# Summing a Mamba scan's states with TensorE transposes instead of identity products, with half the convolution moved to TensorE

## The chip, the cores and the metric

The kernel runs on one core of one Trainium2 chip. The metric is device microseconds from launch to end; the median of three runs of the kernel before is 8551.73 us (8550.24 to 8556.64). One further execution was taken by the hardware profiler, and all durations below are from it.

## The reference

All tensors are float32. The input is 8 images of 256 channels and 32 x 32 pixels, read as 1024 tokens of 256 channels. Four networks follow each other. The first is four Mamba layers and a gate; the other three are attention blocks, which the change does not touch. A Mamba layer is, for each image (cut to what matters):

```python
xin, z = jnp.split(layernorm(xs) @ iw.T, 2, axis=-1)        # 512 channels each
xin = silu(causal_depthwise_conv(xin, cw, K=4) + cb)
proj = xin @ xw.T                                           # 16 for dt, 16 for B, 16 for C
dt = softplus(proj[..., :16] @ dw.T + db)                   # 512 channels
A = -exp(alog)                                              # 512 x 16
def step(h, t):                                             # 1024 tokens, one after the other
    h = h * exp(dt_t[..., None] * A) + (dt_t * x_t)[..., None] * b_t[:, None, :]
    return (h, einsum('bdn,bn->bd', h, c_t))                # sum over the 16 states
y = ys + xin * D
xs = xs + (y * silu(z)) @ ow.T
```

## The kernel before

**Units and steps.** A unit is one layer, one image and one half of its tokens (512 tokens): 4 x 8 x 2 = 64 units, made at lines 510 to 515. A unit's 512 channels are four blocks of 128, taken as two pairs (`q`, blocks `i` = 0 and 1), and its 16 states are eight groups `g` of two (`j`). A step is one `(q, g)`: 16 steps to a unit, 1024 in all. The main loop (lines 587 to 617) writes the work of one step out part by part, in the order of `PARTS` (line 64). Each engine keeps this written order, so an instruction that waits holds back everything behind it on its engine.

**One step.**
- `bx0` and `bx1` (`forced`, lines 472 to 481, one for each block `i`): TensorE spreads `dt * x * B` over the two states. The matrix `dtxT` holds `dt * x` with tokens on the partitions; `dg` holds B as diagonals. The result `bx` (128 channels x 512 tokens x 2 states) has two PSUM buffers of two banks. The array is used as four tiles of 64 x 64: row tile `h` is a half of the tokens, column tile `r` a half of the channels.
- `da0` and `da1` (line 483): ScalarE computes `da = exp(dt * A)` for the next step, two tiles each.
- `state` (line 528): VectorE runs the recurrence with a hardware scan over 512 tokens, one scan for each block and state, four in a step, into `h`.
- `hc` (`product`, line 540): GpSimd multiplies the four state tiles by C, which a DMA has broadcast to all partitions (`ct`, two steps ahead). In the first half of an image VectorE first copies out the last state as the carry.
- `y` (`summed`, lines 492 to 503), three steps later (`LAG_Y`): TensorE sums the states in PSUM. The multiplied states `h` stream as the moving operand against `twin`, two stacked 64 x 64 identities, in the same 64 x 64 tiles. A pair `q` begins with the products `xin * D` through the diagonals `dd`, and both PSUM banks of `y` gather 16 states.
- `z` (`gate`, line 505): after the last group, VectorE multiplies `y` by `silu(z)` into `sz`.

**Beside the scan.** The letters `a` to `d` in `PARTS` are four slots in each step, 64 slots in a unit. `beside` (line 552) puts the segments of five generators there; `BESIDE_SCAN` (lines 66 to 72) lists the slot of each segment. `inward`, two units ahead, is the layer norm, the input projection (products `pin`), the convolution, SiLU and the projection `pp`. `onward`, one unit ahead, makes dt with softplus and `dtx`; `turn` transposes `dtx`; `outward`, one unit behind, is the output projection `po`; `weights` loads a layer. They share two PSUM banks (the tag `mm`, line 97), so a product waits for an earlier one to be read out.

**Convolution.** For each of four blocks, ScalarE takes the last tap out of PSUM with a scale and a bias (line 249), and VectorE adds the three other taps from the same PSUM tile (lines 253 to 255). GpSimd adds the first three tokens' contribution (line 257).

**Softplus.** The kernel computes it as max(v, 0) + log(1 + exp(-|v|)) with a correction for the rounding of 1 + e. ScalarE makes `e`, `one` = 1 + e, `ln` and 1 - `one`; GpSimd then makes three sums of 128 x 1024: `e + (1 - one)`, `+ ln`, `+ dt` (lines 321 to 325).

The prologue (`PROLOGUE`, line 80) does the same stages for the first units in a written order. Later come the attention blocks, from about 6240 us on.

Of the kernel before, what the change touches and what calls it, by code (L numbers as in the profile page):

```python
# [12 lines left out]
F32 = mybir.dt.float32  # L13
# [6 lines left out]
P = 128  # L20
# [6 lines left out]
NG = 2  # L27
# [25 lines left out]
class Engines:  # L53
# [7 lines left out]
LAG_Y = 3  # L61


PARTS = ("ct", "a", "bx0", "da0", "y", "z", "bx1", "da1", "b", "hc", "c", "d")

BESIDE_SCAN = (
    ("weights", 2, (0, 0, 0, 11)),
    ("onward", 1, (1, 8, 8, 8, 8, 13, 19, 25, 27, 31, 35, 35, 41, 45, 46, 51)),
    ("turn", 1, (46, 49, 57, 58)),
    ("outward", -1, (6, 13, 16, 20, 23, 30, 32, 33, 35, 41, 48, 50, 53, 53, 57)),  # L70
    ("inward", 2, (0, 0, 3, 10, 15, 19, 19, 29, 29, 34, 39, 39, 44, 44, 44, 46, 49, 59, 63)),
)

DIAGONALS = (12, 24, 36, 39, 44, 48, 52, 56)

LAST_ON_VECTOR = (2, 1)

PROLOGUE = "WIIWIZZZWIWWIIIIIIIIIIIIIIIJOJOJOGJOJJOGJOOOJOOJJJTGCOGOJOGCGOJJOOTJDGJJJGTJT"  # L80


def mamba_phase(tc, ctx, a, spill, ident, gvec, stats):
# [43 lines left out]
    def weights(s):  # L127

        l = s["l"]
        if (s["b"], s["c"]) != (0, 0):  # L130
            return
        w = layers[l] = {}
        v = w["vec"] = wp.tile([P, V_N], F32, name=f"vec{l}", tag="vec", bufs=2)
        nc.sync.dma_start(v, a["m_vec"][l])
        w["in"] = wp.tile([P, CT, 2 * DI], F32, name=f"win{l}", tag="win")
        nc.sync.dma_start(w["in"], a["m_in"][l])
        yield
        w["A"] = wp.tile([P, DT * DS], F32, name=f"A{l}", tag="A", bufs=2)
        nc.scalar.activation(w["A"], v[:, V_AL:V_AL + DT * DS], AF.Exp)
        nc.scalar.activation(w["A"], w["A"], AF.Identity, scale=-1.0)  # L140
        yield

        w["dd"] = wp.tile([P, DT, H], F32, name=f"dd{l}", tag="dd", bufs=2)
        for j in range(DT):
            nc.gpsimd.tensor_scalar_mul(w["dd"][:, j, :], twin, v[:, V_D + j:V_D + j + 1])
        yield

        ps = ps_m.tile([P, T], F32, name=f"pib{l}", tag="mm")
        for e in range(2 * DT):
            for k in range(CT):  # L150
# [45 lines left out]
    def inward(s):  # L196
# [34 lines left out]
        if c == 0:  # L231
            tail = st["tail"] = wk2.tile([P, DT, K - 1], F32, name=f"tail{u}", tag="tail")
            head = w["head"]
        else:
            tail = st["tail"]
            head = wk1.tile([P, DT, K - 1], F32, name=f"head{u}", tag="head")
            more = wk1.tile([P, DT, K - 1], F32, name=f"more{u}", tag="more")
            nc.gpsimd.tensor_tensor(head, tail, taps[:, :, 0:1].to_broadcast([P, DT, K - 1]), ALU.mult)
            for k in range(1, K - 1):
                n = K - 1 - k  # L240
                nc.gpsimd.tensor_tensor(more[:, :, :n], tail[:, :, k:], taps[:, :, k:k + 1].to_broadcast([P, DT, n]), ALU.mult)
                nc.gpsimd.tensor_tensor(head[:, :, :n], head[:, :, :n], more[:, :, :n], ALU.add)
        xin = s["xin"] = []
        for q in range(DT // 2):
            xin.append(wk5.tile([P, 2, T], F32, name=f"xin{u}_{q}", tag="xin"))
            for i in range(2):
# [33 lines left out]
    def onward(s):  # L280
# [18 lines left out]
        for q in range(DT // 2):  # L299
# [13 lines left out]
            one = wk1.tile([P, 2, T], F32, name=f"one{u}_{q}", tag="one")  # L313
            nc.scalar.activation(one, e, AF.Identity, bias=1.0)
            yield
            ln = wk1.tile([P, 2, T], F32, name=f"ln{u}_{q}", tag="sq")
            nc.scalar.activation(ln, one, AF.Ln)

            nc.scalar.activation(one, one, AF.Identity, scale=-1.0, bias=1.0)
            yield  # L320
            nc.gpsimd.tensor_tensor(e, e, one, ALU.add)
            yield
            nc.gpsimd.tensor_tensor(e, e, ln, ALU.add)
            yield
            nc.gpsimd.tensor_tensor(dt, dt, e, ALU.add)
            yield
# [145 lines left out]
    def forced(s, q, g, i):  # L472

        bx = ps_b.tile([P, T, NG], F32, name=f"bx{s['name']}_{q}_{g}_{i}", tag="bx")
        for k in range(NB):
            for h in range(2):
                for r in range(2):
                    t = h * (T // 2) + k * H
                    nc.tensor.matmul(bx[r * H:(r + 1) * H, t:t + H, :], lhsT=s["dtxT"][q][h * H:(h + 1) * H, i, k, r * H:(r + 1) * H],
                                     rhs=s["dg"][g][h * H:(h + 1) * H, k, :, :], start=True, stop=True)  # L480
        return bx

    def decays(s, q, g, i):
# [8 lines left out]
    def summed(s, q, g, j, h):  # L492

        if g == 0 and j == 0:
            s["y"] = [ps_y.tile([P, T], F32, name=f"y{s['name']}_{q}_{r}", tag=f"y{r}") for r in range(2)]
            for r in range(2):
# [12 lines left out]

    units = []  # L510
    for l in range(NL):
# [75 lines left out]
    for i in range(len(steps) + per_unit):  # L587
# [6 lines left out]
        for part in PARTS:  # L594
# [15 lines left out]
            elif 0 <= i - LAG_Y < len(steps):  # L610
                s, q, g = steps[i - LAG_Y]
                if part == "y":
                    for j in range(NG):
                        summed(s, q, g, j, hs[i - LAG_Y])
                    del hs[i - LAG_Y]
                elif g == NGR - 1:
                    gate(s, q)


ATT_W = ("wq1", "wk1", "wv1", "wo1", "wq2", "wk2", "wv2", "wq3", "wk3", "wv3", "wo3")  # L620
# [601 lines left out]
def layout(i):  # L1222
# [18 lines left out]


    swap = np.arange(DI).reshape(DT // 2, 2, 2, H).transpose(0, 2, 1, 3).reshape(DI)
    m["in_proj_w"] = np.concatenate([m["in_proj_w"][:, :DI], m["in_proj_w"][:, DI + swap]], axis=1)
# [51 lines left out]
```

## Time and profile before

| | |
|---|---|
| median of three runs | 8551.73 us |
| the profiled execution's span, first to last instruction | 8545.1 us |
| TensorE products (PE) busy | 8295.1 us, 97% |
| TensorE weight loads (PEld) busy | 4184.9 us, 49% |
| VectorE (DVE) busy | 7175.6 us, 84% |
| ScalarE (ACT) busy | 5401.4 us, 63% |
| GpSimd (POOL) busy | 6738.1 us, 79% |
| first `bx` product to last `y` product | 106.2 to about 6242 us |

The profile has the span as the execution's only time; the median is 6.6 us above it. All instructions are recorded through one helper, so every line reads L48, and groups are told apart by their tiles: `y<-h,twin` is the product that writes `y` from `h` and `twin`. A float32 product stands as two MATMUL rows, a transposition as one. A form such as `64*64 64x512` is the tile of the array (rows * columns) and then the moving operand (partitions x columns). In a timeline row the two numbers are the start and the time to the last end, and `x16` is how many instructions were merged. Rows overlap: the next group begins while the last products of the one before are still in the array, so the time of a group is read from its start to the next group's start.

### The profile page before, as it was taken

Reading aid. Unit: us, or ns where it says so; the run is one execution under the profiler, and the core shown is the slowest. Engines: PE = TensorE matmul, PEld = TensorE weight load, DVE = VectorE, ACT = ScalarE, POOL = GpSimd, SP = SyncE. Lnnn points to the kernel's source line nnn. Section 1 sums busy time; section 2 is a strip of 40 time slices with the busy share of each in tenths; the row PEclk is TensorE's granted clock in tenths of the full one; section 3 lists DMA queues with packets and bytes.
Section 4 is the critical chain, followed back from the end, with each engine's and each line's share of the span. In section 5 each row is a group of like instructions: output and inputs, shape, how many; then the busy total and the mean of one; then the engine's idle time right before and its main releaser. Section 6 shows DMA issues by size and latency. Waiting matters only on the chain.

```text
span 8545.1 us, 226062 instructions
## 1 busy us (share of the span) xinstructions
PE 8295.1 (97%) x98322; PEld 4184.9 (49%) x98322; DVE 7175.6 (84%) x7069; ACT 5401.4 (63%) x7613; POOL 6738.1 (79%) x2339
## 2 busy tenths in 40 slices
PE   7999999999999999999999999999989999999998
PEld 4555555555555555555555555555533333333332
DVE  5999999999999999999999999999964555665566
ACT  6777777777777777777777777777632344333434
POOL 5999999999999999999999999999912343334435
PEclk9999999999999999999999999999999999999999
DMA  3444444444443444444444444444410000000000
GB/s 117 128 130 129 129 130 134 132 129 128 128 130 127 135 128 133 128 130 129 128 129 131 130 138 135 141 143 138 142 62 5 9 6 7 10 6 6 1 6 11
DMA packets 558021, 841.07 MB, mean 98 GB/s; under 512 B 311329, under 2 KB 312417, under 8 KB 556385
## 3 DMA queue, kind: packets, MB, share of 16 engines
q1 hardware_dynamic: 556736, 825.47, 31.6%
q8 instruction: 780, 12.78, 0.6%
q14 instruction: 217, 1.77, 0.1%
q10 hardware_dynamic: 288, 1.05, 0.0%
HBM read 771.31 MB, written 55.05 MB: 97 GB/s over the span
## 4 chain that ended last, share of the span: by engine, by line
PE 88%; DVE 6%; ACT 2%; issue 2%; POOL 1%; DMA 0%; SPq 0%; DVEq 0%; POOLq 0%; ACTq 0%
PE bx L48 21%; PE y L48 20%; PE pin L48 11%; PE fs L48 8%; PE fo L48 7%; PE po L48 5%; DVE h L48 4%; PE pp L48 3%; PE fwq L48 2%; PE fwv L48 2%; PE pd L48 2%; PE pvar L48 1%; PE fwk L48 1%; PE pmu L48 1%; PE fpo L48 1%
## 5 line engine op out<-in xcount | busy, mean ns | idle before, releaser
L48 POOL TENSOR_TENSOR h<-h,ct 128x2048 f32<-128x2048 f32 x1022 | 4637.7, 4560 | 169.1 <-DVE hc L48 80.4
L48 ACT ACTIVATE da<-dt,A 128x512 f32<-128x512 f32 x4096 | 2644.6, 715 | 267.2 <-DVE h L48 266.3
L48 PEld LDWEIGHTS bx<-dg,dtxT 64*64 64x64 f32 x65536 | 1889.7, 133 | 1268.8 <-issue 1128.1
L48 DVE TENSOR_TENSOR_SCAN h<-da,hc,bx 128x512 f32<-128x512 f32 x2048 | 2454.7, 1261 | 61.4 <-PE bx L48 29.4
L48 DVE TENSOR_TENSOR_SCAN h<-da,bx 128x512 f32<-128x512 f32 x2048 | 2354.9, 1204 | 95.8 <-PE bx L48 76.8
L48 PE MATMUL bx<-dg,dtxT 64*64 64x128 f32 x65536 | 2222.0, 272 | 64.3 <-DVE h L48 34.7
L48 PE MATMUL y<-h,twin 64*64 64x512 f32 x16384 | 1956.0, 590 | 7.9 <-DVE h L48 4.7
L48 ACT ACTIVATE fp<-fs 128x1024 f32<-128x1024 f32 x768 | 746.3, 1022 | 1117.3 <-PE fs L48 1110.5
L48 PE MATMUL pin<-xn,win 128*128 128x512 f32 x2048 | 1004.9, 614 | 58.8 <-ACT sz L48 48.2
L48 PEld LDWEIGHTS y<-h,twin 64*64 64x64 f32 x16384 | 614.1, 133 | 631.2 <-issue 617.1
L48 POOL TENSOR_TENSOR fz<-fp,fp 128x1024 f32<-128x1024 f32 x48 | 121.9, 2540 | 979.1 <-ACT fp L48 979.1
L48 POOL TENSOR_TENSOR fz<-fz,fp 128x1024 f32<-128x1024 f32 x224 | 586.7, 2622 | 336.6 <-ACT fp L48 332.6
L48 PE MATMUL fo<-fp,fv 128*32 128x512 f32 (+2 forms) x3584 | 781.3, 608 | 4.0 <-ACT fp L48 2.6
L48 DVE TENSOR_TENSOR fz<-fz,fp 128x1024 f32<-128x1024 f32 x384 | 616.8, 1606 | 118.5 <-ACT fp L48 100.7
L48 DVE SCALAR_TENSOR_TENSOR xin<-pin,vec,xin 128x509 f32<-128x509 f32 (+2 forms) x768 | 572.3, 746 | 60.1 <-ACT tail L48 21.2
L48 PE MATMUL fs<-fq,fk 32*128 32x512 f32 (+1 forms) x3072 | 582.2, 634 | 4.1 <-ACT fp L48 2.5
L48 PEld LDWEIGHTS pin<-xn,win 128*128 128x128 f32 x2048 | 349.5, 190 | 423.0 <-issue 281.6
L48 PE MATMUL po<-sz,wo 128*128 128x512 f32 x1024 | 484.1, 605 | 0.8 <-DVE sz L48 0.8
L48 PEld LDWEIGHTS fo<-fp,fv 128*32 128x32 f32 (+2 forms) x3584 | 191.5, 127 | 515.1 <-issue 469.5
L48 ACT ACTIVATE sz<-pin,ib 128x512 f32<-128x512 f32 x256 | 176.0, 688 | 418.3 <-PE pin L48 418.3
L48 ACT ACTIVATE xin<-pin,cb,vec 128x512 f32<-128x512 f32 x256 | 199.2, 778 | 286.0 <-PE pin L48 285.9
L48 POOL TENSOR_TENSOR e<-e,one 128x1024 f32<-128x1024 f32 x128 | 304.5, 2379 | 84.7 <-ACT one L48 81.1
(143 smaller groups left out, 7416.0 us busy)
## 6 DMA issues: line engine op xcount, KB each, us to landing
ct<-cdr SPq DMA_DIRECT2D x1024, 512.0 KB
dg<-diagonals SPq DMA_DIRECT2D x512, 256.0 KB
spill<-xo SPq DMA_DIRECT2D x63, 512.0 KB
x<-spill SPq DMA_DIRECT2D x48, 512.0 KB
xo<-spill SPq DMA_DIRECT2D x48, 512.0 KB
x<-in_x SPq DMA_DIRECT2D x16, 512.0 KB
res<-in_x SPq DMA_DIRECT2D x16, 512.0 KB
diagonals<-bt SPq DMA_DIRECT2D x512, 4.0 KB
```

Of the source, the lines that this page charges most:

```text
L48: return self.tc.keep_in_program_order(getattr(self.engine, name)(*args, **kwargs))
```

## The change

- **States summed by transposes.** `summed` now makes the multiplied states the stationary operand (64 rows of channels, 128 tokens as columns) and streams the 64 x 64 identity past it with `is_transpose`, adding in PSUM. The sum stands with tokens on the partitions: for each state 4 token blocks x 2 blocks `i` x 2 row tiles `r` = 16 transposes. The `xin * D` products take the same shape, with `xin` stationary.
- **Turned back.** After the last group, a new `leave` (part `z`) copies both banks of `y` to SBUF with ScalarE, and `gate` (new part `g`) turns them back by eight 128 x 128 transposes into the same two PSUM banks before VectorE's multiplication.
- **`bx` in 64 x 128 tiles.** `forced` issues one product over all 128 channels where it issued two over 64 each.
- **Half of the convolution on TensorE.** For `q` = 0 (`CONV_Q` = 1) ScalarE copies both projected blocks to SBUF, and four taps are products with diagonal matrices `taps` (made once a layer by GpSimd), shifted in the output columns, into two `mm` banks at once; ScalarE takes the sums out. The second half's first tokens use the kept `past`. The weights' order of channels is changed to fit.
- **Softplus.** `ln` goes to PSUM, 512 tokens at a time, and VectorE adds it to `dt`; GpSimd keeps two of its three sums. `one` uses the buffer `sq`.
- **Order.** `PARTS`, the slots of all stages, those of the DMAs that load the diagonals, and the prologue are new.

```diff
-PARTS = ("ct", "a", "bx0", "da0", "y", "z", "bx1", "da1", "b", "hc", "c", "d")
+CONV_Q = 1
+PARTS = ("bx0", "y", "ct", "z", "g", "da0", "bx1", "a", "da1", "b", "c", "hc", "d")

-    ("onward", 1, (1, 8, 8, 8, 8, 13, 19, 25, 27, 31, 35, 35, 41, 45, 46, 51)),
-    ("turn", 1, (46, 49, 57, 58)),
-    ("outward", -1, (6, 13, 16, 20, 23, 30, 32, 33, 35, 41, 48, 50, 53, 53, 57)),
-    ("inward", 2, (0, 0, 3, 10, 15, 19, 19, 29, 29, 34, 39, 39, 44, 44, 44, 46, 49, 59, 63)),
+    ("onward", 1, (0, 3, 9, 9, 13, 14, 21, 28, 29, 38, 43, 43, 46, 48, 50, 63)),
+    ("turn", 1, (42, 51, 60, 63)),
+    ("outward", -1, (2, 9, 12, 16, 16, 20, 25, 29, 30, 33, 43, 47, 48, 48, 56)),
+    ("inward", 2, (5, 5, 15, 21, 21, 25, 27, 32, 39, 41, 41, 47, 47, 47, 49, 49, 54, 55, 59)),
-DIAGONALS = (12, 24, 36, 39, 44, 48, 52, 56)
+DIAGONALS = (21, 28, 29, 33, 37, 48, 60, 61)

+        w["taps"] = wp.tile([P, 2 * CONV_Q, K, H], F32, name=f"taps{l}", tag="taps")
+        for j in range(2 * CONV_Q):
+            for k in range(K):
+                nc.gpsimd.tensor_scalar_mul(w["taps"][:, j, k, :], twin, v[:, V_CW + j * K + k:V_CW + j * K + k + 1])
...
+            if q < CONV_Q:
+                raw = xin[q]
+                for i in range(2):
+                    j = 2 * q + i
+                    ps = in_proj(j)
+                    nc.scalar.activation(raw[:, i, :], ps, AF.Identity, bias=w["ib"][:, j:j + 1])
+                    yield
+                conv = [ps_m.tile([P, T], F32, name=f"conv{u}_{q}_{r}", tag="mm") for r in range(2)]
+                def tap(k, to, source, stop=False):
+                    for r in range(2):
+                        for i in range(2):
+                            nc.tensor.matmul(conv[r][i * H:(i + 1) * H, to], lhsT=w["taps"][r * H:(r + 1) * H, 2 * q + i, k, :],
+                                             rhs=source(slice(r * H, (r + 1) * H), i), start=(k == K - 1 and to.start == 0), stop=stop)
...
+                for n in range(K):
+                    tap(K - 1 - n, slice(n, T), lambda rows, i: raw[rows, i, :T - n], stop=(c == 0 and n == K - 1))
+                    if n == 1:
+                        yield
+                if c:
+                    past = st["past", q]
+                    for n in range(1, K):
+                        tap(K - 1 - n, slice(0, n), lambda rows, i: past[rows, i, K - 1 - n:], stop=(n == K - 1))
+                for r in range(2):
+                    nc.scalar.activation(xin[q][:, r, :], conv[r], AF.Identity, bias=w["vec"][:, V_CB + 2 * q + r:V_CB + 2 * q + r + 1])
+                yield
+                continue
...
-            ln = wk1.tile([P, 2, T], F32, name=f"ln{u}_{q}", tag="sq")
-            nc.scalar.activation(ln, one, AF.Ln)
+            for r in range(2):
+                ln = ps_m.tile([P, T], F32, name=f"ln{u}_{q}_{r}", tag="mm")
+                nc.scalar.activation(ln, one[:, r, :], AF.Ln)
+                nc.vector.tensor_tensor(dt[:, r, :], ln, dt[:, r, :], ALU.add)
+                yield
...
-            nc.gpsimd.tensor_tensor(e, e, ln, ALU.add)
...
-                for r in range(2):
-                    t = h * (T // 2) + k * H
-                    nc.tensor.matmul(bx[r * H:(r + 1) * H, t:t + H, :], lhsT=s["dtxT"][q][h * H:(h + 1) * H, i, k, r * H:(r + 1) * H],
-                                     rhs=s["dg"][g][h * H:(h + 1) * H, k, :, :], start=True, stop=True)
+                t = h * (T // 2) + k * H
+                nc.tensor.matmul(bx[:, t:t + H, :], lhsT=s["dtxT"][q][h * H:(h + 1) * H, i, k, :], rhs=s["dg"][g][h * H:(h + 1) * H, k, :, :],
+                                 start=True, stop=True)
...
-                    nc.tensor.matmul(s["y"][r][i * H:(i + 1) * H, :], lhsT=s["w"]["dd"][r * H:(r + 1) * H, 2 * q + i, :],
-                                     rhs=s["xin"][q][r * H:(r + 1) * H, i, :], start=True, stop=False)
+                    for r in range(2):
+                        nc.tensor.matmul(s["y"][r][:, k, i, :], lhsT=s["xin"][q][r * H:(r + 1) * H, i, k * P:(k + 1) * P],
+                                         rhs=s["w"]["dd"][r * H:(r + 1) * H, 2 * q + i, :],
+                                         start=(k == 0 and i == 0), stop=False, skip_group_check=True)
+        last = g == NGR - 1 and j == NG - 1
+        for k in range(NB):
+            for i in range(2):
+                for r in range(2):
+                    nc.tensor.matmul(s["y"][r][:, k, i, :], lhsT=h[r * H:(r + 1) * H, i, j, k * P:(k + 1) * P], rhs=twin[r * H:(r + 1) * H, :],
+                                     is_transpose=True, start=False, stop=(last and k == NB - 1 and i == 1), skip_group_check=True)
+    def leave(s, q):
+        s["yt"] = wk1.tile([P, 2, NB, P], F32, name=f"yt{s['name']}_{q}", tag="res")
         for r in range(2):
-            for i in range(2):
-                nc.tensor.matmul(s["y"][r][i * H:(i + 1) * H, :], lhsT=twin[r * H:(r + 1) * H, :], rhs=h[r * H:(r + 1) * H, i, j, :],
-                                 start=False, stop=(g == NGR - 1 and j == NG - 1))
+            nc.scalar.copy(s["yt"][:, r, :, :].rearrange("p b t -> p (b t)"), s["y"][r].rearrange("p b i t -> p (b i t)"))
 
     def gate(s, q):
         for r in range(2):
             z = s["sz"][:, 2 * q + r, :]
-            nc.vector.tensor_tensor(z, s["y"][r], z, ALU.mult)
+            back = ps_y.tile([P, NB, P], F32, name=f"back{s['name']}_{q}_{r}", tag=f"y{r}")
+            for k in range(NB):
+                nc.tensor.transpose(back[:, k, :], s["yt"][:, r, k, :], ident)
+            nc.vector.tensor_tensor(z, back.rearrange("p b t -> p (b t)"), z, ALU.mult)
```

More of the change, by code (lines that the diff above doesn't have):

```diff
@@ L237, in inward @@
             more = wk1.tile([P, DT, K - 1], F32, name=f"more{u}", tag="more")
-            nc.gpsimd.tensor_tensor(head, tail, taps[:, :, 0:1].to_broadcast([P, DT, K - 1]), ALU.mult)
+            J = slice(2 * CONV_Q, DT)
+            N = DT - 2 * CONV_Q
+            nc.gpsimd.tensor_tensor(head[:, J, :], tail[:, J, :], taps[:, J, 0:1].to_broadcast([P, N, K - 1]), ALU.mult)
             for k in range(1, K - 1):
                 n = K - 1 - k
-                nc.gpsimd.tensor_tensor(more[:, :, :n], tail[:, :, k:], taps[:, :, k:k + 1].to_broadcast([P, DT, n]), ALU.mult)
-                nc.gpsimd.tensor_tensor(head[:, :, :n], head[:, :, :n], more[:, :, :n], ALU.add)
+                nc.gpsimd.tensor_tensor(more[:, J, :n], tail[:, J, k:], taps[:, J, k:k + 1].to_broadcast([P, N, n]), ALU.mult)
+                nc.gpsimd.tensor_tensor(head[:, J, :n], head[:, J, :n], more[:, J, :n], ALU.add)
         xin = s["xin"] = []
@@ L245, in inward @@
             xin.append(wk5.tile([P, 2, T], F32, name=f"xin{u}_{q}", tag="xin"))
+            if q < CONV_Q:
[11 more added lines that the diff above has]
+                                             rhs=source(slice(r * H, (r + 1) * H), i), start=(k == K - 1 and to.start == 0), stop=stop)
+                if c == 0:
+                    past = st["past", q] = wk2.tile([P, 2, K - 1], F32, name=f"past{u}_{q}", tag=f"past{q}")
+                    nc.scalar.copy(past, raw[:, :, T - K + 1:])
+                for n in range(K):
[10 more added lines that the diff above has]
+                continue
             for i in range(2):
@@ L312, in onward @@
             nc.scalar.activation(e, e, AF.Exp, scale=-1.0)
[L313 removed]
+            one = wk1.tile([P, 2, T], F32, name=f"one{u}_{q}", tag="sq")
             nc.scalar.activation(one, e, AF.Identity, bias=1.0)
             yield
[L316 to L317 removed]
+            for r in range(2):
+                ln = ps_m.tile([P, T], F32, name=f"ln{u}_{q}_{r}", tag="mm")
+                nc.scalar.activation(ln, one[:, r, :], AF.Ln)
+                nc.vector.tensor_tensor(dt[:, r, :], ln, dt[:, r, :], ALU.add)
+                yield
             nc.scalar.activation(one, one, AF.Identity, scale=-1.0, bias=1.0)
[L320 removed]
             nc.gpsimd.tensor_tensor(e, e, one, ALU.add)
[L322 to L323 removed]
             yield
@@ L494, in summed @@
         if g == 0 and j == 0:
-            s["y"] = [ps_y.tile([P, T], F32, name=f"y{s['name']}_{q}_{r}", tag=f"y{r}") for r in range(2)]
-            for r in range(2):
+            s["y"] = [ps_y.tile([P, NB, 2, H], F32, name=f"y{s['name']}_{q}_{r}", tag=f"y{r}") for r in range(2)]
+            for k in range(NB):
                 for i in range(2):
-                    nc.tensor.matmul(s["y"][r][i * H:(i + 1) * H, :], lhsT=s["w"]["dd"][r * H:(r + 1) * H, 2 * q + i, :],
-                                     rhs=s["xin"][q][r * H:(r + 1) * H, i, :], start=True, stop=False)
+                    for r in range(2):
[10 more added lines that the diff above has]
+        s["yt"] = wk1.tile([P, 2, NB, P], F32, name=f"yt{s['name']}_{q}", tag="res")
         for r in range(2):
-            for i in range(2):
-                nc.tensor.matmul(s["y"][r][i * H:(i + 1) * H, :], lhsT=twin[r * H:(r + 1) * H, :], rhs=h[r * H:(r + 1) * H, i, j, :],
-                                 start=False, stop=(g == NGR - 1 and j == NG - 1))
+            nc.scalar.copy(s["yt"][:, r, :, :].rearrange("p b t -> p (b t)"), s["y"][r].rearrange("p b i t -> p (b i t)"))
     def gate(s, q):
@@ L507, in gate @@
             z = s["sz"][:, 2 * q + r, :]
-            nc.vector.tensor_tensor(z, s["y"][r], z, ALU.mult)
+            back = ps_y.tile([P, NB, P], F32, name=f"back{s['name']}_{q}_{r}", tag=f"y{r}")
+            for k in range(NB):
+                nc.tensor.transpose(back[:, k, :], s["yt"][:, r, k, :], ident)
+            nc.vector.tensor_tensor(z, back.rearrange("p b t -> p (b t)"), z, ALU.mult)
     units = []
@@ L616, in mamba_phase @@
                 elif g == NGR - 1:
-                    gate(s, q)
+                    (leave if part == "z" else gate)(s, q)
 ATT_W = ("wq1", "wk1", "wv1", "wo1", "wq2", "wk2", "wv2", "wq3", "wk3", "wv3", "wo3")
@@ L1243, in layout @@
     swap = np.arange(DI).reshape(DT // 2, 2, 2, H).transpose(0, 2, 1, 3).reshape(DI)
-    m["in_proj_w"] = np.concatenate([m["in_proj_w"][:, :DI], m["in_proj_w"][:, DI + swap]], axis=1)
+    part = np.concatenate([swap[:2 * P * CONV_Q], np.arange(2 * P * CONV_Q, DI)])
+    m["in_proj_w"] = np.concatenate([m["in_proj_w"][:, part], m["in_proj_w"][:, DI + swap]], axis=1)
+    m["conv_w"] = m["conv_w"][:, part]
     m["out_proj_w"] = m["out_proj_w"][:, :, swap]
```

4 lines of the change are left out of this document (2 added, 2 removed).

## The prediction

> **What bounds the kernel now.** I read the page's busy table, then one window from the middle of the scan, then TensorE's timeline, then what TensorE waited for. The page gives TensorE 97%, but this includes the attention blocks. The stretch that the change touches is 1000:5500 (columns: length, then busy time of PE, PEld, DVE, ACT, POOL, then clock):
>
> ```profile
> 1000.00:5500.00 4500.00, 4433.15 (x65211) 2467.72 (x65213) 4245.53 (x4332) 3317.19 (x4919) 4337.13 (x1476) 1.00 0.43 131
> ```
>
> TensorE is busy 98.5%, GpSimd 96.4%, VectorE 94.3%, ScalarE 73.7%, at full clock. GpSimd ran 751 state products there, so a step is 5.99 us and a unit 95.9 us; 64 units after the first `bx` at 106 us end near 6242 us.
>
> ```profile
> 3036.16 1.10 PE L48 MATMUL bx<-dg,dtxT 64*64 64x128 f32 x32
> 3037.08 1.90 PE L48 MATMUL y<-h,twin 64*64 64x512 f32 x16
> 3038.80 1.05 PE L48 MATMUL bx<-dg,dtxT 64*64 64x128 f32 x32
> 3039.96 1.96 PE L48 MATMUL pin<-xn,win 128*128 128x512 f32 x4
> 3042.69 1.98 PE L48 MATMUL pin<-xn,win 128*128 128x512 f32 x4 [0.78 <-ACT sz L48]
> 3044.61 1.10 PE L48 MATMUL bx<-dg,dtxT 64*64 64x128 f32 x32
> 3045.53 1.04 PE L48 MATMUL y<-xin,dd 64*64 64x512 f32 x8
> 3046.39 1.90 PE L48 MATMUL y<-h,twin 64*64 64x512 f32 x16
> 3048.11 1.05 PE L48 MATMUL bx<-dg,dtxT 64*64 64x128 f32 x32
> 3049.09 0.66 PE L48 MATMUL pt<-ident,dtx 128*128 128x128 f32 x4
> ```
>
> The groups stand back to back. From start to start: `bx` 0.92, `y` 1.72 (four rounds of 0.43), `bx` 0.98 where another tile shape follows, `xin * D` 0.86, four transpositions 0.49. Only one wait, 0.78 us, is marked. Its total, with the next largest:
>
> ```profile
> PE pin L48 <- ACT sz L48: 36.6, 47, 0.8
> PE bx L48 <- DVE h L48: 13.8, 51, 0.5
> ```
>
> Over 47 units that is 1.1 us in 95.9. TensorE's work sets the pace, and a saving elsewhere buys at most this 1.1 us. GpSimd (92.4 us a unit) and VectorE (90.5) stand close behind.
>
> **The change part by part, in us of TensorE per unit.** Weight loads price most of it. The first two rows are loads for transpositions; the third is products that move a single column, so that their spacing is that of a plain load:
>
> ```profile
> 2597.53 0.32 PEld L48 LDWEIGHTS pb<-ident,proj 16*128 16x128 f32 x4 [0.17 <-ACT da L48]
> 3049.09 0.42 PEld L48 LDWEIGHTS pt<-ident,dtx 128*128 128x128 f32 x4 [0.17 <-DVE h L48]
> 2990.20 3.63 PE L48 MATMUL pib<-vec,win 128*128 128x1 f32 x32
> 2993.76 1.10 PE L48 MATMUL bx<-dg,dtxT 64*64 64x128 f32 x32
> ```
>
> A load of 128 columns for a transposition follows the last one after (0.32 - 0.137)/3 = 0.061 us (0.137 is one load). A plain float32 load of 128 columns takes (2993.76 - 2990.20)/32 = 0.111. A transposition moving 128 columns takes 0.109 (the `pt` group less its first, exposed load), so moving 64 takes 0.055.
>
> 1. *State sums.* 2 states x 16 transposes are 16 pairs a step, the two row tiles of a pair side by side, as the four tiles are now. A pair costs the larger of its load (0.061) and its product (0.055): I take 0.06. 16 x 0.06 = 0.96, plus 0.05 because `bx`'s plain load no longer fits under the last product: 1.01 in place of 1.72. Over 16 steps **-11.3**. Ends: 0.055 a pair, 1.3 better; 0.111 (loads as slow as plain ones), 13 worse. `pb` has the same tile width and the same kind of load, so I stay near it.
> 2. *`bx` in pairs.* 256 rounds as before, but the load is 0.111 against 0.109 for the product: +0.002 to 0.003 each, +0.7. The first load after a change of tile shape lies open: `pin` x4 takes 1.98 after such a change and 1.88 without, 0.10 for 128 columns, and half of it now for 64; +0.05 x 16 = +0.8. Together **+1.5**; ends 0 and +3.3 (a pair costing 0.007 more).
> 3. *`xin * D`.* 32 instructions, 16 pairs at the plain load's 0.111 = 1.78 against 0.86, twice: **+1.8**.
> 4. *Turning back.* Eight transpositions 0.87, two changes of shape at 0.09 each, and open loads of 0.1: 1.15, twice: **+2.3**.
> 5. *Waiting for the copy.* `z` and `g` stand together, so TensorE holds `bx1` and all behind it while ScalarE copies. `dtxT<-pt` shows the chain: last transposition to its result 0.27, 0.04 to the copy's start, 0.59 the copy; with 0.05 back, 0.9 before the first four can start, and the second copy lets the other four wait another 0.1: **+2.0** for two pairs. Ends: 1.6, and 5.8 if ScalarE were each time in the 1.9 us SiLU of `sz`. `da0` now follows the copies on ScalarE, and VectorE's gate follows `back`; both have room (ScalarE 26%; VectorE's scans of `bx0`, 2.3 us, run meanwhile).
> 6. *Convolution.* Four taps x 2 rounds x 0.43 = 3.44; the three short products of a second half, 6 rounds of about 0.06, in every second unit 0.18; two visits in another tile shape 0.4: **+4.0**.
>
> Sum: -11.3 + 1.5 + 1.8 + 2.3 + 2.0 + 4.0 = **+0.3**.
>
> VectorE loses six convolution passes (0.75 each) and gains four sums (nearest row: `sz<-y,sz`, 0.67): -1.8. GpSimd loses two 2.38 us sums and the `head` edge: -5.0. ScalarE gains four copies (0.59) and two conv read-outs (0.69): +3.8 on 70.7. None of them sets the pace now, and after it VectorE stands at 88.7 and GpSimd at 87.4, so this buys nothing until TensorE has fallen to some 89 us.
>
> *New waits.* VectorE's sum waits for `ln` in ScalarE's order and holds the next scans; `bx` is two buffers ahead, so VectorE's 5.4 idle us cover it. The sum also holds an `mm` bank, and the convolution holds both from slot 32 to 39: in that stretch `onward` (38) and `outward` (33, done by 16 outside the last layer) ask for none. After `ln` (slot 43) the next `mm` product is in slot 47, one step later. `pp` comes one step after the SiLU as now. Slots in GpSimd's queue: `hc` moves behind slot `c`, and the three steps until `y` cover it. SP's queue: `ct` is still sent two steps ahead and the diagonals of the next unit before it begins; DMA share is 43%. I put the change in waits at **+0.3**, between -1.1 (all gone) and +2.0 (two more waits as long as one scan pair can make them). Prologue: eight products of 0.5 on GpSimd and another order, taken as 0, between -5 and +15 us in all.
>
> So **+0.6 us a unit, x 64 = +38 us**. On the profiled span of 8545.1 this is 8583; the median lies 6.6 above the span, so **8590 us**.
>
> [...]
>
> **Rivals.**
> - *The loads hide better (faster).* If a pair of state transposes costs 0.055 (product alone, `pt`'s price per column), step 1 gains 1.3: 0.6 - 1.3 = -0.7, 8507 us. It decides from 0.0577 down (0.6 / 256 below 0.06). For it: `pt`'s loads vanish under 0.109 products. Against: 0.061 in `pb`, and loads of both tiles go on at once. With `bx` at 0.109 as well, -1.4 and 8460. Should all of TensorE's old waits go too, -2.8 and 8370.
> - *Waits take the place of the sum (slower).* Two copies behind a busy ScalarE (+3.8), or `mm` waits of a scan pair twice a unit: +2.5 to +4.5, 8700 to 8850. Against: slots leave a step between holders.
> - *Transposing loads at the plain price, or row tiles not side by side (much slower).* +13 a unit, 9400 us. Against: `pb`; `bx`'s four loads now fit under 0.109.
> - *GpSimd or VectorE take over:* at 89 us a unit, 8110 us; no sum here comes near it, TensorE's best being 95.9 + 0.3 - 1.3 - 1.5 - 0.4 - 1.1 = 91.9 with every bound in its favour.
>
> **How the numbers follow.** Near balance as summed, 8535 to 8700: 0.49. Loads hide better: 0.38. Waits: 0.09. Plain price: 0.04. The range takes the first case's upper bounds (pairs of `bx` 0.007 dearer, or waits +2) to 8700 and the second's to 8430. A measurement here can tell 0.2% (17 us). The first case's lower part, near 8551, and a part of the second's give "same" 0.11; faster 0.40; slower 0.49.
>
> **What would show it.** Right: `y` groups of about 1.0 us start to start with 32 rows; `bx` groups 0.92 to 1.0; two gaps of about 0.9 us a unit ahead of `back`; PE still 97 to 99% busy at 1000:5500 and GpSimd near 91%, VectorE 92%. Wrong: `y` spacing away from 0.06; a clock below 1.00; PE idle on `mm` readers (ACT or DVE) beyond 3 us a unit; a step set by VectorE or GpSimd.

## The result and the profile after

The median of twenty runs is 8565.9 us (8555.7 to 8569.9), against 8550.7 us (8545.1 to 8556.6) for the kernel before, also over twenty runs. The ratio is 1.0017 with a 95% interval of 1.0010 to 1.0023. The kernel is 15 us slower. The sign of the likeliest case was right, its +38 us more than twice too large, and the centre lies inside the 0.2% that I had called "same". The profiled span is 8564.1 us, 19.0 above that of before.

The page after, its busy table:

```profile
span 8564.1 us, 206743 instructions
PE 8299.7 (97%) x88850; PEld 5192.3 (61%) x88850; DVE 7041.0 (82%) x6941; ACT 5553.7 (65%) x8093; POOL 6442.0 (75%) x2179
```

TensorE's busy time is the same as before (8295.1) with different work inside it. VectorE lost 135 us, GpSimd 296 us; neither loss reached the end time. The scan stretch 1000:5500 by windows (columns as before: length, busy time of PE, PEld, DVE, ACT, POOL, clock, DMA share, GB/s):

```profile
1000.00:5500.00 4500.00, 4422.50 (x57985) 3196.99 (x57984) 4126.51 (x4215) 3408.96 (x5239) 4102.30 (x1355) 0.99 0.44 130
```

TensorE 98.3%, VectorE 91.7%, GpSimd 91.2%: the shares that the prediction named (97 to 99, 92, 91). TensorE's timeline of the kernel after, some 15 us later than where the prediction looked at before's:

```profile
3050.86 1.95 PE L48 MATMUL conv<-xin,taps 64*64 64x512 f32 x16
3052.74 1.16 PE L48 MATMUL bx<-dg,dtxT 64*128 64x128 f32 x16
3053.73 1.16 PE L48 MATMUL y<-twin,h 64*128 64x64 f32 x32
3054.72 1.12 PE L48 MATMUL bx<-dg,dtxT 64*128 64x128 f32 x16
3055.77 1.94 PE L48 MATMUL conv<-xin,taps 64*64 64x510 f32 x16
3057.64 1.16 PE L48 MATMUL bx<-dg,dtxT 64*128 64x128 f32 x16
3058.64 1.17 PE L48 MATMUL y<-twin,h 64*128 64x64 f32 x32
3060.47 1.15 PE L48 MATMUL back<-ident,yt 128*128 128x128 f32 x8 [0.67 <-ACT yt L48]
3061.55 0.72 PE L48 MATMUL bx<-dg,dtxT 64*128 64x128 f32 x8
```

From start to start: `y` 0.99 with 32 rows (was 1.72), `bx` 0.99 ahead of `y` (was 0.92) and 1.03 ahead of another tile shape (was 0.98), a convolution visit 1.88, `back` 1.08. Ahead of `back` stands the wait for ScalarE's copy. The two largest waits of TensorE in 1000:5500, after:

```profile
PE back L48 <- ACT yt L48: 62.5, 92, 1.1
PE pib L48 <- DVE dt L48: 6.5, 3, 2.2
```

The wait of `pin` for `sz` (36.6 us before) and that of `bx` for `h` (13.8) are gone. The last line stands for only three events, and much of the result hangs on it.

**Where the time went.** I took each unit's length from one first scan to the next, and each group of TensorE's work from its start to the next group's start, for twelve regular units of layer 2, its third to its fourteenth (us a unit):

| tile | before | after | change | forecast |
|---|---|---|---|---|
| `y` with the wait ahead of `back` | 27.47 | 18.05 | -9.42 | -11.3 + 2.0 |
| `bx` | 30.83 | 33.30 | +2.47 | +1.5 |
| `xin * D` | 1.72 | 3.47 | +1.75 | +1.8 |
| `back` | 0 | 2.15 | +2.15 | +2.3 |
| `conv` | 0 | 3.89 | +3.89 | +4.0 |
| `pin` | 16.04 | 14.53 | -1.51 | } |
| all others | 19.47 | 20.11 | +0.64 | } +0.3 |
| sum | 95.53 | 95.50 | -0.02 | +0.6 |

A regular unit is as long as before, but this hides a loss of clock. Five of the twelve units last 1.5 us longer than their neighbours (96.65 against 95.12, or 96.1 against 94.6). In each of these five, and in none of the other seven, the trace's record of the granted clock has one stretch of 3.4 us at half speed, shortly after the unit's first scan, behind the products `pb` and `pd`. The unit just ahead of the twelve shows one too (windows with the columns as above, then TensorE's timeline):

```profile
3283.00:3293.10 10.10, 10.10 (x152) 7.61 (x151) 8.27 (x9) 10.09 (x18) 9.73 (x3) 1.00 0.43 144
3293.10:3296.50 3.40, 3.40 (x52) 3.40 (x50) 3.01 (x4) 3.40 (x7) 3.09 (x2) 0.51 0.36 105
```
```profile
3291.14 1.70 PE L48 MATMUL pd<-proj,wdt 16*128 16x512 f32 x3
3292.77 1.78 PE L48 MATMUL bx<-dg,dtxT 64*128 64x128 f32 x16
3294.33 1.92 PE L48 MATMUL y<-twin,h 64*128 64x64 f32 x32
3296.04 1.36 PE L48 MATMUL bx<-dg,dtxT 64*128 64x128 f32 x16
```

`y` takes 1.71 here in place of 0.99, and the two `bx` groups 1.56 and 1.29 in place of 0.99 and 1.03, though TensorE had no pause. In the table this is 0.35 us of `bx` and 0.29 of `y`. From the second unit to the sixty-first, the three that load weights left out, there are 23 such stretches in 57 units. At 1.5 us each that is some 35 us, an estimate, and more than the whole difference of 15. The kernel before has none in these units.

Since the regular units balance, the 19.0 us of the span show up elsewhere, and they can be added up: first scan +4.4 (the prologue), layer 0 +7.7, layer 1 +11.1, layer 2 +7.6, layer 3 -12.8, after the last scan +1.0. In layers 0 to 2 one unit, the fifteenth, in which the next layer's weights are loaded, went from 99.0, 99.0 and 102.3 to 107.4, 109.0 and 108.9: +25 us together, almost the whole growth of these three layers. This is the stage (windows 2990:3008, 3008:3026 and 3026:3044 after, columns as above):

```profile
2990.00:3008.00 18.00, 15.55 (x164) 10.40 (x161) 15.43 (x17) 14.13 (x25) 17.95 (x15) 0.91 0.55 109
3008.00:3026.00 18.00, 17.23 (x140) 15.78 (x142) 5.40 (x7) 8.62 (x13) 8.41 (x10) 0.62 0.29 106
3026.00:3044.00 18.00, 18.00 (x212) 12.01 (x210) 16.54 (x20) 8.76 (x15) 15.39 (x4) 1.00 0.37 119
```

The clock is 0.62 in the middle window. TensorE's timeline there, after:

```profile
3004.60 1.98 PE L48 MATMUL po<-sz,wo 128*128 128x512 f32 x4
3008.77 6.05 PE L48 MATMUL pib<-vec,win 128*128 128x1 f32 x32 [2.18 <-DVE dt L48]
3014.76 2.08 PE L48 MATMUL bx<-dg,dtxT 64*128 64x128 f32 x16
3016.62 3.52 PE L48 MATMUL y<-dd,xin 64*128 64x64 f32 x32
3019.93 1.92 PE L48 MATMUL y<-twin,h 64*128 64x64 f32 x32
3021.63 2.00 PE L48 MATMUL bx<-dg,dtxT 64*128 64x128 f32 x16
3023.56 1.98 PE L48 MATMUL po<-sz,wo 128*128 128x512 f32 x4
3025.48 1.16 PE L48 MATMUL bx<-dg,dtxT 64*128 64x128 f32 x16
```

And VectorE's:

```profile
3008.03 0.69 DVE L48 TENSOR_TENSOR dt<-ln,dt 128x512 f32<-128x512 f32 x1 [0.90 <-ACT ln L48]
3016.95 2.33 DVE L48 TENSOR_TENSOR_SCAN h<-da,bx 128x512 f32<-128x512 f32 x2 [8.16 <-PE bx L48]
```

The product `pib` (slot 11 of the unit) needs an `mm` bank. One was held by `po` from slot 9, the other by the first `ln` of the new softplus, also slot 9, which is free only when VectorE has added it at 3008.03. TensorE stands still for 2.18 us and then runs at half speed: `pib` takes 6.0 us where before it took 3.56 in the row that the prediction shows, `bx` 1.86 in place of 0.99, `xin * D` 3.3 in place of 1.73.

### The profile page after: what moved, and what is told of

It is laid out like the page before. It is cut to its first block, busy times and chain, and to the rows that moved or that the text cites. A ratio compares the mean times of both kernels' runs of the same rounds, so it can differ in the third digit from the quotient of the medians.

```text
span 8564.1 us, 206743 instructions
## 1 busy us (share of the span) xinstructions
PE 8299.7 (97%) x88850; PEld 5192.3 (61%) x88850; DVE 7041.0 (82%) x6941; ACT 5553.7 (65%) x8093; POOL 6442.0 (75%) x2179
## 4 chain that ended last, share of the span: by engine, by line
PE 90%; ACT 5%; DVE 3%; issue 1%; POOL 1%; DMA 0%; SPq 0%; DVEq 0%; POOLq 0%; ACTq 0%
PE bx L48 23%; PE y L48 14%; PE pin L48 11%; PE fs L48 8%; PE fo L48 7%; PE po L48 6%; PE conv L48 3%; PE pp L48 3%; PE fwq L48 2%; PE fwv L48 2%; PE pd L48 2%; PE back L48 2%; PE pvar L48 1%; PE pt L48 1%; PE fwk L48 1%
## 5 line engine op out<-in xcount | busy, mean ns | idle before, releaser
L48 PEld LDWEIGHTS bx<-dg,dtxT 64*128 64x128 f32 x32768 | 2028.7, 190 | 692.9 <-issue 602.5
L48 PE MATMUL bx<-dg,dtxT 64*128 64x128 f32 x32768 | 2371.6, 285 | 30.3 <-DVE h L48 17.6
L48 PE MATMUL y<-twin,h 64*128 64x64 f32 x32768 | 1212.0, 225 | 11.2 <-DVE h L48 5.8
L48 PEld LDWEIGHTS y<-twin,h 64*128 64x128 f32 x32768 | 1182.9, 142 | 11.9 <-DVE h L48 6.2
L48 PE MATMUL pin<-xn,win 128*128 128x512 f32 x2048 | 967.2, 610 | 11.0 <-DVE xin L48 3.6
L48 PEld LDWEIGHTS fs<-fq,fk 32*128 32x128 f32 (+1 forms) x3072 | 182.5, 185 | 371.4 <-issue 242.1
L48 DVE RECIPROCAL frec<-fzs 128x512 f32<-128x512 f32 x64 | 214.9, 3358 | 142.9 <-PE fzs L48 142.9
```

Source lines behind the costliest of these rows:

```text
L48: return self.tc.keep_in_program_order(getattr(self.engine, name)(*args, **kwargs))
```

## The experiments

Theory A, after the result: TensorE's order of work sets the pace, and what the change lost is `pib`'s wait, with the half clock behind it, and the wait for the copy. Its rivals: another engine sets the pace in a regular unit, so that what TensorE is spared comes back as a new wait; or the transposed sums are not worth what their groups' lengths say.

**1. `pib` in a later slot**, when both banks of `ln` are long free.

```diff
-    ("weights", 2, (0, 0, 0, 0, 11)),
+    ("weights", 2, (0, 0, 0, 0, 18)),
```

> The changed kernel, with the last segment of the weights stage (the 32 one-column products pib) in slot 18 in place of 11. In the changed kernel the three units that load a layer's weights last 107.4, 109.0 and 108.9 us, against 95.6 for the others (before: 99.0, 99.0, 102.3). Theory A: there pib waits for a PSUM bank that the new ln holds until VectorE has added it, TensorE stands still for 2.2 us and then runs at half clock (granted 0.62 at 3008 to 3026 us); with both banks free at slot 18 the three units come to 97 to 100 us and the time to 8535 to 8547 us, below the kernel before. Theory B: GpSimd's eight new products for taps (3.3 us at slot 0) and the weights' DMA cost it; they stay where they are, so the units stay at 106 to 109 us and the time at 8560 to 8570.

Measured: 8538.6 us, ratio to the kernel before 0.9986 (0.9977 to 0.9995), 27 us below the kernel after. `pib` follows `po` without a gap and runs at full speed:

```profile
3003.93 3.70 PE L48 MATMUL po<-sz,wo 128*128 128x512 f32 x8
3007.47 3.63 PE L48 MATMUL pib<-vec,win 128*128 128x1 f32 x32
```

Layers 0 to 2 are shorter by 12.5, 10.5 and 10.4 us, layer 3, which loads no next layer, is unchanged (1517.0 and 1516.9). The three weight units now last 100.2 us each, which is 24.9 us of the 33.4, and the half speed at `pib` lasts 3.4 us in each of them where it lasted 13.7, 13.7 and 10.2. With the other 8.5 us go five half-speed stretches fewer in regular units (18 for 23). One number in the slot table turns the change from slower to slightly faster, so the loss of the three weight units is shown to come from `pib`'s place; that it waited for the bank that `ln` held is what its releaser (`dt`, the sum that reads `ln`) says.

**2. Turning back one part later**, so that `bx1` runs while ScalarE copies.

```diff
-PARTS = ("bx0", "y", "ct", "z", "g", "da0", "bx1", "a", "da1", "b", "c", "hc", "d")
+PARTS = ("bx0", "y", "ct", "z", "da0", "bx1", "g", "a", "da1", "b", "c", "hc", "d")
```

> The changed kernel, with part g (the turning back and VectorE's gate) behind bx1 in place of ahead of da0. Theory A (TensorE's work sets the pace in the regular units): the wait for ScalarE's copy, 0.83 us twice a unit ahead of back, lies under bx1 (1.04 us), and a change of tile shape is saved: 1.7 to 2.0 us a unit, 64 units, so 8440 to 8470 us. Theory B (another engine or another wait is as close): the regular unit falls by less than 0.6 us, because VectorE's gate now comes behind the scans of bx1 and the next D products wait for their banks, or because the scans stay late: 8530 to 8570 us.

Measured: 8523.4 us, ratio 0.9966 (0.9954 to 0.9979). The regular unit falls by 0.75 us, to 94.75, less than half of what A expected. The wait ahead of `back` is gone, but a new one appeared, the one that B named (its range was missed by 7 us): the first `xin * D` products of the next pair overwrite the bank that VectorE's gate reads, and the gate now stands behind two more scans (see run 8). `xin * D` rose by 0.52 and the `bx` ahead of it by 0.53.

**3. Both edits.**

```diff
-PARTS = ("bx0", "y", "ct", "z", "g", "da0", "bx1", "a", "da1", "b", "c", "hc", "d")
+PARTS = ("bx0", "y", "ct", "z", "da0", "bx1", "g", "a", "da1", "b", "c", "hc", "d")
-    ("weights", 2, (0, 0, 0, 0, 11)),
+    ("weights", 2, (0, 0, 0, 0, 18)),
```

> Both edits: pib in slot 18, part g behind bx1. If the two causes are apart from each other (theory A of both), the gains add: 25 us and 110 us, so 8410 to 8450 us. If only pib's wait matters: 8530 to 8545. If neither: 8560 to 8570.

Measured: 8501.7 us, ratio 0.9944 (0.9930 to 0.9957). Against the kernel after -64 us; the two alone gave -27 and -42. They nearly add, and the expected 8410 to 8450 was missed for the reason seen in run 2.

**4. The convolution back on VectorE**, everything else as after.

```diff
-CONV_Q = 1
+CONV_Q = 0
```

> The changed kernel, with CONV_Q = 0: the whole convolution back on VectorE, no diagonal taps; all else, the slots too, as in the changed kernel. TensorE loses 3.9 us of products a unit, VectorE gains six passes (4.5 us) on 88. Theory A (TensorE sets the pace): the unit falls from 95.5 to 92 to 94 us, 8350 to 8470 us. Theory B (VectorE was the next bound, or its passes hold the mm banks and TensorE waits for them): within 1 us of 95.5 or above, 8500 to 8650 us.

Measured: 8735.0 us, ratio 1.0212 (1.0198 to 1.0226). TensorE has 3.9 us less to do in a unit and the unit grows from 95.50 to 98.45. By windows 3400:4300 of this kernel, and what its TensorE waits for there:

```profile
3400.00:4300.00 900.00, 855.63 (x10967) 626.37 (x10963) 845.77 (x879) 653.15 (x1007) 803.66 (x264) 0.97 0.43 126
```
```profile
PE bx L48 <- DVE h L48: 20.3, 25, 1.3
PE back L48 <- ACT yt L48: 16.2, 18, 1.2
PE pin L48 <- DVE dt L48: 4.3, 9, 0.7
```

The time lies above both ranges. No engine is full: VectorE 94%, TensorE 95%. TensorE idles 4.7 us a unit, 3.2 more than after, and 2.2 of it is `bx` waiting for VectorE's scans to free its buffers. The clock falls too, to 0.97 on average: the twelve units have 19 stretches at half speed where the kernel after has five, and `pd`, which waits for almost nothing, takes 5.10 us a unit in place of 2.64. So the conclusion that TensorE's work alone sets the pace falls here, but the 2.95 us are two losses, a late VectorE and a slower clock. They also depend on the place: in layer 1 a unit of this run takes 97.3. The slots were made for the other convolution, and what it would cost on VectorE with slots of its own was not run.

**5. The sums and `bx` as before**, the convolution, softplus and order as after: `summed`, `gate` and `forced` are those of before, and nothing is turned back.

```diff
-                    nc.tensor.matmul(s["y"][r][:, k, i, :], lhsT=h[r * H:(r + 1) * H, i, j, k * P:(k + 1) * P], rhs=twin[r * H:(r + 1) * H, :],
-                                     is_transpose=True, start=False, stop=(last and k == NB - 1 and i == 1), skip_group_check=True)
...
+                nc.tensor.matmul(s["y"][r][i * H:(i + 1) * H, :], lhsT=twin[r * H:(r + 1) * H, :], rhs=h[r * H:(r + 1) * H, i, j, :],
+                                 start=False, stop=(g == NGR - 1 and j == NG - 1))
```

> The changed kernel with the sums of the states, the D products, the gate and bx's tiles as before (products with twin, 64 x 64 tiles, no turning back); the convolution on TensorE, the softplus and all slots as changed. Theory A (TensorE's pieces simply add up): y +9.4, D -1.75, back -2.15, bx -2.5 us a unit by the two traces, so +3.0 x 64 = +195 us on 8566: 8730 to 8790. Theory B (the gain of the transposes was eaten by another engine's limit, so taking them out costs less): 8600 to 8680.

Measured: 8671.8 us, ratio 1.0143 (1.0128 to 1.0159).

```profile
3400.00:4300.00 900.00, 900.00 (x13191) 494.66 (x13184) 820.09 (x840) 653.96 (x994) 805.63 (x254) 1.00 0.43 127
```

TensorE does not pause at all, and a unit takes 97.33 us. So the convolution, the softplus and the new order without the sums cost 97.33 - 95.53 = +1.80 us a unit, and the sums with `bx` in pairs and the turn give 95.50 - 97.33 = -1.83. The two halves of the change cancel. The time lies in B's range, but not for B's reason, since no other engine holds TensorE up: the pieces do add up, as A has it, only to 1.83. `y` (+9.42), `xin * D` (-1.75) and `back` (-2.15) return as expected, but `bx` gives 3.09 where 2.5 was taken, `conv` 0.31 and `pd` 0.29 where nothing was. There are 28 changes of tile shape a unit here and 36 after, and none of the regular units loses clock. The clock loss at `pib` is here too (weight units 106.8 against 97.4, a standstill of 2.49 us), so it comes without transposed sums too.

**6. One sum of softplus from GpSimd to VectorE in the kernel before.**

```diff
-            nc.gpsimd.tensor_tensor(e, e, ln, ALU.add)
+            nc.vector.tensor_tensor(dt, dt, ln, ALU.add)
```

> The kernel before with one edit: the sum with ln is made by VectorE (dt + ln, 128 x 1024, from SBUF, about 1.2 us) and no longer by GpSimd (2.38 us). GpSimd loses 4.8 us a unit. Theory A (TensorE sets the pace in layers 0 to 2, GpSimd only in layer 3, where the output gate's sums come on top): units of layers 0 to 2 stay within 0.3 of 95.5 us, those of layer 3 fall from 96.6 by 1 us or more: 8525 to 8548 us. Theory B (GpSimd is as close everywhere): more than 0.7 us a unit in all layers, below 8505. Theory C (VectorE's new sum holds scans up): above 8555.

Measured: 8656.4 us, ratio 1.0124 (1.0108 to 1.0139). A unit grows by 1.45 us to 96.97, as C had it.

```profile
3400.00:4300.00 900.00, 876.24 (x12936) 489.58 (x12932) 863.89 (x876) 657.01 (x972) 818.36 (x261) 1.00 0.43 127
```

VectorE stands at 96%, TensorE has fallen from 98.6 to 97.4%, GpSimd from 96.4 to 90.9%. Relief of GpSimd bought nothing, in layer 3 either, where A expected it: its regular units went from 96.70 to 100.07. VectorE's 5.4 idle us a unit in the kernel before were not free: two more sums a unit cost 1.45, and 1.27 of it is TensorE's idle time ahead of `bx`, which went from 0.51 to 1.78 us a unit.

**7. `bx` in four 64 x 64 tiles again**, all else as after (`forced` of before).

```diff
-                nc.tensor.matmul(bx[:, t:t + H, :], lhsT=s["dtxT"][q][h * H:(h + 1) * H, i, k, :], rhs=s["dg"][g][h * H:(h + 1) * H, k, :, :],
-                                 start=True, stop=True)
+                for r in range(2):
+                    nc.tensor.matmul(bx[r * H:(r + 1) * H, t:t + H, :], lhsT=s["dtxT"][q][h * H:(h + 1) * H, i, k, r * H:(r + 1) * H],
+                                     rhs=s["dg"][g][h * H:(h + 1) * H, k, :, :], start=True, stop=True)
```

> The changed kernel with bx in four tiles of 64 x 64 as before, all else as changed, so that the shape of the tiles changes between bx and the transposes, twice more in a step. Theory A: a change of shape costs 0.09 us and an open load of 0.05 or 0.1; two more a step cost 4.5 to 6 us a unit and the quads give back 2.5: 8690 to 8800 us. Theory B (the change between these two shapes costs little): the 2.5 us come back, 8400 to 8480 us.

Measured: 8626.9 us, ratio 1.0091 (1.0075 to 1.0106); a unit takes 96.48 us, +0.98. The `bx` groups fall by only 0.32, while the `y` groups rise by 1.65 and `xin * D` by 0.20, because every step now changes the array's shape twice between `bx` and `y`: 62 changes a unit instead of 36. This run has no half-speed stretch in a regular unit, and the kernel after has (0.35 us in `bx`, 0.29 in `y`); against full clock the narrower `bx` tiles bring nothing, and the 26 changes cost 1.6 us in all. The pairs cost `bx` 2.5 us against before but are worth having beside transposed sums. The sign was as A had it, the size about half.

**8. The gate ahead of the scans of `bx1`**, on top of run 3. TensorE's order stays; VectorE multiplies by the gate before, not after, the scans of the step's second block.

```diff
-PARTS = ("bx0", "y", "ct", "z", "da0", "bx1", "g", "a", "da1", "b", "c", "hc", "d")
+PARTS = ("bx0", "y", "ct", "z", "da0", "bx1", "a", "da1", "b", "c", "hc", "d")
...
-                if 0 <= i < len(steps):
-                    k = int(part[2])
-                    state(i, k, forced(*steps[i], k))
+                k = int(part[2])
+                bx = forced(*steps[i], k) if 0 <= i < len(steps) else None
+                if k == 1 and 0 <= i - LAG_Y < len(steps) and steps[i - LAG_Y][2] == NGR - 1:
+                    gate(*steps[i - LAG_Y][:2])
+                if bx is not None:
+                    state(i, k, bx)
```

> On top of pib in slot 18 and the turning back behind bx1 (8502 us): VectorE's gate is written ahead of the scans of bx1, TensorE's order unchanged. Theory A (what is left of the wait is that the next D products wait 0.52 us a unit for the gate, and bx 0.5): both go, 8440 to 8485 us. Theory B (VectorE, now waiting for the turned sums, brings its scans late instead): 8495 to 8530 us.

Measured: 8392.3 us, ratio 0.9814 (0.9800 to 0.9827), 1.9% faster than the kernel before and better than either theory had it. TensorE's timeline behind `back` in run 3:

```profile
3448.73 1.09 PE L48 MATMUL back<-ident,yt 128*128 128x128 f32 x8
3449.66 1.88 PE L48 MATMUL po<-sz,wo 128*128 128x512 f32 x4
3451.47 1.16 PE L48 MATMUL bx<-dg,dtxT 64*128 64x128 f32 x16
3453.41 0.43 PE L48 MATMUL y<-dd,xin 64*128 64x64 f32 x2 [0.78 <-DVE sz L48]
3454.01 1.88 PE L48 MATMUL y<-dd,xin 64*128 64x64 f32 x29 [0.16 <-DVE sz L48]
```

and in run 8:

```profile
3482.60 1.09 PE L48 MATMUL back<-ident,yt 128*128 128x128 f32 x8
3483.53 1.88 PE L48 MATMUL po<-sz,wo 128*128 128x512 f32 x4
3485.34 1.16 PE L48 MATMUL bx<-dg,dtxT 64*128 64x128 f32 x16
3486.33 1.90 PE L48 MATMUL y<-dd,xin 64*128 64x64 f32 x32
3488.07 1.16 PE L48 MATMUL y<-twin,h 64*128 64x64 f32 x32
```

`bx` to `xin * D` is 1.94 in the one and 0.99 in the other. VectorE's rows give the reason: in run 3 the gate stands behind four scans, in run 8 behind two, where `back` has just ended.

```profile
3447.99 4.78 DVE L48 TENSOR_TENSOR_SCAN h<-da,hc,bx 128x512 f32<-128x512 f32 x4
3452.70 1.26 DVE L48 TENSOR_TENSOR sz<-back,sz 128x512 f32<-128x512 f32 x2
```
```profile
3481.69 2.32 DVE L48 TENSOR_TENSOR_SCAN h<-da,bx 128x512 f32<-128x512 f32 x2
3483.93 1.26 DVE L48 TENSOR_TENSOR sz<-back,sz 128x512 f32<-128x512 f32 x2
3485.11 2.32 DVE L48 TENSOR_TENSOR_SCAN h<-da,bx 128x512 f32<-128x512 f32 x2
```

A regular unit falls from 94.48 to 92.88: `bx` -0.83, `xin * D` -0.52, `y` -0.22. About 1.25 of it is at this place, where one pair of each unit waited. TensorE is idle 0.15 us a unit, with VectorE 94.5% busy (850.33 of 900 us in 3400:4300).

## Why the prediction was right or wrong

- *What bounds the kernel.* Half right. TensorE's work is what a regular unit's length is made of (idle 1.3 us before, 1.5 after). But "a saving elsewhere buys at most this 1.1 us", read backwards, let me cost every other engine's change at nothing. Run 6 shows VectorE as a second bound (+1.45 us a unit for two sums of 1.2), and run 4 points the same way, mixed there with a loss of clock.
- *Step 1, state sums,* and *step 5, the copy.* Right: -9.42 together against -9.3, with 0.29 of half clock in it. A `y` group takes 0.99 (forecast 1.01), a pair of transposes 0.062 (0.99/16; forecast 0.06), the wait 0.67 and 0.84 with its neighbours (0.9). The rival of better-hidden loads (0.055, from 0.0577 down) fell, and so did the one of the plain price.
- *The price of a load.* The plain loads of `bx` repeat at 0.112 a pair, near the 0.111 of `pib` before; the float32 loads for transposing repeat at 0.062 a pair, near the 0.061 of `pb` before. The row of `pb` was the right one to sum by.
- *The granted clock,* which was in no term. The clock in 1000:5500 fell to 0.99, one of the prediction's own signs of being wrong. Besides the weight units it is half speed in 23 regular units, for 3.4 us each. Runs 5 and 7 have none of these stretches: run 5 sums by products with `bx` in four tiles, run 7 by transposes with `bx` in four tiles. So transposed sums alone do not bring them; with `bx` in pairs beside them, every run has such stretches, run 8 too (0.99 in 4900:5900), where TensorE is idle only 0.15 us a unit. What the clock answers to stays open.
- *Step 2, `bx`.* Mis-sized: +2.47, not +1.5, and 0.35 of it is half clock. A group ahead of `y` takes 0.995: its pairs follow each other at 0.112, but the second stands 0.213 behind the first, so that 0.10, about one load (0.111), lies open. In a group behind `y` (1.04) the second pair stands 0.165 behind the first, and the next shape begins 0.09 later than another pair would. I had let half a load lie open, at every second group only. Its upper bound, +3.3, held it.
- *Steps 3, 4 and 6.* Right: 1.75, 2.15 and 3.89 against 1.8, 2.3 and 4.0.
- *New waits, +0.3: the step that failed.* In a regular unit the sign was wrong: the old wait of `pin` (0.83) left and its visits fell from seven to five, so `pin` and all others together changed by -0.87, near the lower bound of -1.1. In the weight-loading units it was wrong the other way: I looked for holders of `mm` banks at slots 32 to 43 and never set the first `ln` (slot 9) against `pib` (slot 11). A wait of 2.2 us was within what I allowed; the longer half clock behind it, which makes it 8 us, was in no term. Run 1 shows this loss.
- *Prologue,* 0 (-5 to +15): +4.4.
- *Layer 3,* which I took to be like the others, is 12.8 us shorter. It was not like them before: its regular units (the third to the thirteenth) lasted 96.70 us, against 95.53 in layers 1 and 2, and after the change they last 95.50. The gain of 1.2 us a unit is there in run 1 too (95.63), and about half of it in runs 5 and 7, whose units of layer 3 last 97.96 and 97.12, still some 0.6 longer than their other units. Only in layer 3 does GpSimd make two more sums of 2.39 us per image, and it was 97.2% busy in 4700:5900 before and 93.0% after; so GpSimd may have set the pace there. Run 6, which relieved it, could not show that, since VectorE lengthened these units. The cause stays open.
- *The sum.* 64 units at +0.6 were to give +38. In a regular unit the waits came out 1.17 below their term and `bx` 0.97 above its own, so that the -0.02 owes as much to luck as to the sum. The runs show 45 regular units of layers 0 to 2 at about 0, three weight units at +8 and a layer 3 at -13. That the total came out slower is due to the three weight units, as run 1 shows; without the half clock in the regular units, some 35 us by the estimate above, it would have come out faster as well. The sign was right by luck.
- *Rivals.* That waits take the place of the sum was nearest in kind, in three units and not in each. That GpSimd or VectorE take over was set aside since no sum reached 89; runs 4 and 6 show VectorE holding TensorE up at 97 to 98, and run 8 reaches 92.9 with VectorE at 94.5% and TensorE hardly waiting.

## What to carry to other kernels

Price a change in every stage that shares its buffers, not only in the stage that repeats most: set the holders of each shared bank side by side by slot, also for the stage that runs once a layer. An engine at 94% can already be a bound (run 6: +1.45 us a unit), so work shifted to it is not free even where another stands at 98%; the share alone does not tell, since in run 8 VectorE is as busy and TensorE hardly waits. When an engine waits on a reader, look first at what stands ahead of that reader in its own queue: moving VectorE's gate ahead of two scans bought 109 us, about as much as the transposed sums bring in all (1.83 us x 64 = 117). And look at the granted clock also where an engine never pauses: a mean of 0.99 hid 23 stretches at half speed.

## What the runs showed of the hardware

- The granted clock can fall to half while TensorE is busy without a pause: 10.10 of 10.10 us busy at 1.00 in 3283.00:3293.10, then 0.51 in 3293.10:3296.50. Such a stretch of 3.4 us made a unit 1.5 us longer; there are 23 in 57 regular units after, none before and none in runs 5 and 7.
- The 32 one-column products `pib` behind a standstill of 2.2 us went with 10.2 to 13.7 us at half speed in the kernel after (`bx` 1.86 for 0.99; clock 0.62 in 3008:3026), and behind one of 2.49 us in run 5 with 6.8. Without a standstill they went with 3.4 us in run 1 and with none, none and 6.8 us in the three layers before. So a standstill is not needed, and with one the half speed mostly lasted longer.
- A pair of float32 state transposes repeats every 0.062 us although each of its loads has 128 columns, while products that load as many columns and move a single one (`pib`) repeat every 0.111 us: in these runs loads for transposing follow each other at 0.56 of the spacing of plain ones.
- Changing the array's tile shape has a price: 26 more changes a unit in run 7 made the unit 0.98 us longer (1.6 against full clock), in spite of narrower tiles of `bx` that load half as many columns. In the kernel after, the last row of `po` or `pin` ahead of `bx` takes 0.52 us to the next start, where it takes 0.43 ahead of another row of its own.
